# Layer 0's background steps re-spaced, and layer 1's first two convolution sums issued high products first

## The chip, the cores and the metric

The kernel runs on one core of a Trainium2 chip. The metric is the device time of one execution in microseconds (us). The profile has six rows of engines: PE (TensorE, matrix products), PEld (its weight loads), DVE (VectorE), ACT (ScalarE), POOL (GpSimd), and SP (SyncE, which here only issues transfers). Each works through its own list of instructions in order.

## The reference

Four layers on `x` of 16 images, 256 channels, 28x28 pixels. Only layers 0 and 1 matter here.

```python
# layer 0
out = _binary_activation(x)                       # the sign of x
scaling = mean(abs(weights), axis=(1, 2, 3))
bw = sign(weights)
y = _sat_conv2d(out, bw, padding=1) * scaling     # 3x3 convolution
yn = (y - mean(y)) * rsqrt(var(y) + EPS) * gamma + beta   # over all 16 images
x = yn + x
# layer 1
residual = prelu(x, a_alpha1)
z = hardsign(x + a_move)
y = conv_general_dilated(z, clip(a_w, -1, 1), padding=1)  # 3x3 convolution
y = prelu(bn(y, a_bn1), a_alpha2)
...                                               # gate, bn, 1x1 convolution, gate, bn
```

The normalization of layer 0 needs the mean and variance over all images. So layer 1 cannot begin before layer 0's last image has been convolved, evacuated and counted.

## The kernel before

**Layer 0** is `sign_layer` (line 322 on). Its blocks are images 0 to 14 whole and image 15 in three parts, a half and two quarters (15a, 15b, 15c). For a block j the kernel issues, in a hand-written order that holds for PE, ACT, DVE and SP alike:

1. `products(j)`: 36 matmuls of 392 columns for a whole image (line 340), on two weight rows packed into one value;
2. `sign_image(j+1)`: ACT writes the signs of the next image into one of two padded buffers `fpads` (line 451, two instructions), and SP issues the load of image j+4 (line 444; four buffers `xs`);
3. `post(j-1)`: DVE takes the statistics of the image before (line 598, four instructions), and POOL stores its integers `n` to memory (line 600);
4. two *slots* for a whole image, one for each part of image 15, from image 1 on: each slot takes the next entry of the list `steps`, and first runs what the entry before left over (`late`);
5. `apart(j)`: ACT rounds the sum in PSUM (lines 351 and 352), DVE separates the two packed rows (line 354). PSUM has three buffers for such sums.

The statistics of the first images are merged (`gather`, line 167) in the body of the first block whose part number is over 26, which is image 14.

**The list `steps`** is background work for later. Six times four entries prepare layer 1's and layer 2's weights: *taps* (DVE, lines 503 and 134, sums of three filter taps), *high* (ACT, line 514, four conversions to 16 bit; what it leaves over is *low*, line 518, four DVE instructions), *sum* (ACT, lines 285 and 288: absolute sum and sign sum of layer 0's weights; the last one leaves over the final sum on DVE, lines 294 and 295), and *sign* (ACT, line 266; leaves over one DVE instruction, line 267). Then comes *fw* (DVE line 302, ACT line 303, DVE line 134: layer 1's 1x1 weights), and `constants` (line 547 on): some 30 small DVE instructions and one ACT square root that fold layer 1's normalizations, and eight small SP loads of the gates' weights. Each of these entries issues the load of the entry two places further on (`load_ahead`); these loads share three buffers.

That is 26 entries. Images 1 to 14 and the three parts of image 15 have 2x14 + 3 = 31 slots. The entries therefore sit in the slots of images 1 to 13: odd images hold taps and high, even images sum and sign, image 13 holds fw and constants.

**Between the layers** `keep_busy(28)` (line 432) lets PE run 28 products on a buffer of zeros. `norm` (lines 184 and 134 to 148) makes scale and shift, `enter` (line 669, DVE) applies them to image 0, `sign1` (line 675, ACT) takes signs, `transform` (line 134, DVE, output `vs16`) makes the four row combinations u = 0 to 3 of a fast convolution in 16 bit, and `widen` (line 695, ACT) copies them to 32 bit (`vs`).

**Layer 1's convolution** is `conv` (line 713): for one u, six matmuls with the 16-bit *high* part of the weights on `vs16`, then six with the 32-bit *low* part on `vs`. `iteration(b)` begins with `conv_pair` for u = 1 and u = 2.

Of the kernel before, what the change touches and what calls it, by code (L numbers as in the profile page):

```python
# [34 lines left out]
ALU = mybir.AluOpType  # L35
# [8 lines left out]
HN = N // 2  # L44
# [39 lines left out]
def forward(ctx: ExitStack, tc: tile.TileContext, d: dict, out: bass.AP, careful: bool):  # L84
# [4 lines left out]
    V, A, T = nc.vector, nc.scalar, nc.tensor  # L89
# [11 lines left out]
    def pv(name):  # L101
        return vec[:, VECS.index(name), :]
# [30 lines left out]
    def tt(o, a, b, op):  # L133
        V.tensor_tensor(o, a, b, op)  # L134
        return o

    def rsqrt(name, v, half=None):

        r, t = (const.tile(list(v.shape), F32, name=name + q) for q in ("_r", "_t"))
        A.activation(t, v, AF.Sqrt)  # L140
        V.reciprocal(r, t)
        tt(t, r, r, ALU.mult)
        if half is not None:
            tt(r, r, half, ALU.mult)
        else:
            V.tensor_scalar(r, r, -0.5, None, ALU.mult)
        tt(t, t, v, ALU.mult)
        V.scalar_tensor_tensor(r, t, -3.0, r, ALU.add, ALU.mult)
        return r
# [98 lines left out]
    def load_ahead(steps, n, now=True):  # L248

        for s in steps[:n] if now else ():  # L250
            s.load()
        return [lambda s=s, t=t: (s.work(), t.load() if t else None)[0] for s, t in zip(steps, steps[n:] + [None] * n)]
# [143 lines left out]
    def combine(name, a, f, c=0.0):  # L396

        v = vtile(name)
        V.tensor_scalar(v, a, f, c, ALU.mult, ALU.add)
        return v  # L400
# [19 lines left out]
    with tc.tile_pool(name="ps_conv", bufs=3, space=PSUM) as psc, \  # L420
            tc.tile_pool(name="ps_sm", bufs=2, space=PSUM) as pss:

        def conv_ps():
            return psc.tile([P, 2, 512], F32, tag="cv", name="cv")
# [9 lines left out]
        with tc.tile_pool(name="ph1", bufs=1) as ph:  # L434
# [4 lines left out]
            def load_x(b, integers=False, rows=((0, S),)):  # L439
                if not xs[b]:  # L440
                    xs[b] = ph.tile([P, 2, N], F32, tag="xs", name=f"xs{b}", bufs=4)
                for r0, r1 in rows:
                    n = slice(r0 * S, r1 * S)
                    nc.sync.dma_start(out=xs[b][:, :, n], in_=d["x"][b][:, :, n])
                if integers:
                    ns[b] = ph.tile([P, 2, N], I16, tag="n", name=f"n{b}", bufs=2)
                    nc.sync.dma_start(out=ns[b], in_=n0d[b])
# [43 lines left out]
            w1 = [ph.tile([P, 2, 3, 4, 256], dt, name=f"w1_{i}") for i, dt in enumerate((HI, FR))]  # L491
# [32 lines left out]
            def fw_step():  # L524
                sts = []

                def load():
                    sts.append(xpool.tile([P, 3, 256], F32, tag="x2", name="stf", bufs=3))
                    nc.sync.dma_start(out=sts[0][:, 0:2, :], in_=d["fw"])

                return Step(load, lambda: split2(fw, sts[0][:, 0:2, :]))
# [5 lines left out]
            c1, c2, c3, c4 = (c_bn[:, i, :] for i in range(4))  # L537
            cc, zb2 = vtile("cc"), vtile("zb2")
            ra1, ra2, rf2, us1, ns1 = (vtile(q) for q in ("ra1", "ra2", "rf2", "us1", "ns1"))
            mix_x, mix_y, mix_c = (const.tile([P, 2, 2], F32, name=n) for n in ("mix_x", "mix_y", "mix_c"))  # L540
# [6 lines left out]
            def constants():  # L547
                for p in pads:
                    nc.gpsimd.memset(p, 0.0)
                nc.gpsimd.tensor_copy(  # L550
                    doubts[:, 4 * NB:4 * NB + 6], vec[:, VECS.index("a1"):VECS.index("a3") + 1, :].rearrange("p i k -> p (i k)")
                )
                for i, n in enumerate(("a_alpha2", "f_alpha2")):
                    nc.gpsimd.tensor_copy(doubts[:, 4 * NB + 6 + 2 * i:4 * NB + 8 + 2 * i], pv(n))
                v = const.tile([P, 4, 2], F32, name="v_bn")
                for i, bn in enumerate(bns):
                    V.tensor_scalar(v[:, 2 * i:2 * i + 2], bn[:, 3::4], EPS, None, ALU.add)
                r = rsqrt("bn", v)
                for i, bn in enumerate(bns):
                    two = slice(2 * i, 2 * i + 2)  # L560
                    tt(s_bn[:, two], bn[:, 0::4], r[:, two], ALU.mult)
                    tt(c_bn[:, two], bn[:, 2::4], s_bn[:, two], ALU.mult)
                    tt(c_bn[:, two], bn[:, 1::4], c_bn[:, two], ALU.subtract)
                tt(cc, c2, c4, ALU.add)

                for o, q in ((ra1, "a_alpha1"), (ra2, "a_alpha2"), (rf2, "f_alpha2")):
                    V.tensor_scalar(o, pv(q), -1.0, 1.0, ALU.mult, ALU.add)
                V.tensor_scalar(us1, s1, 1.0 / UP, None, ALU.mult)
                V.tensor_scalar(ns1, s1, -1.0 / UP, None, ALU.mult)
                tt(zb2, c2, pv("f_move"), ALU.add)  # L570
                for g, (q, scale) in enumerate((("a", pv("a_scale")), ("f", pv("f_scale")))):
                    V.tensor_scalar(mix_x[:, g], scale, 1.0 / N, None, ALU.mult)
                    V.tensor_scalar(mix_y[:, g], scale, -1.0 / N, 1.0 / N, ALU.mult, ALU.add)
                    rows = slice(32 * g, 32 * g + 32)
                    nc.sync.dma_start(out=w_1[:, :, rows], in_=d[f"se1_{q}"])
                    nc.sync.dma_start(out=w_2[rows], in_=d[f"se2_{q}"])
                    nc.sync.dma_start(out=b_1[rows], in_=d[f"seb_{q}"])
                    nc.sync.dma_start(out=w_2[64 + 32 * g:65 + 32 * g], in_=d[f"seb2_{q}"])
                tt(mix_c[:, 1], pv("f_scale"), c2, ALU.mult)

            w2a = packed_weights(wpool, tag="wa2")

# [3 lines left out]
            signs2, sums0 = sign_weights(xpool, w2a, d["w2a"], ("x2", 3), tmp=ph), weight_sums(room_sums, d["w0_rows"], sf0, 0)  # L586
            w1_steps = [w1_step(k, c) for k in range(2) for c in range(3)]
            ahead = load_ahead([t for s, *three in zip((w for w, _, _ in w1_steps), sums0, signs2) for t in (s, *three)] + [fw_step()], 2)
            steps = []
            for (_, high, low), taps, add_up, sign in zip(w1_steps, ahead[0::3], ahead[1::3], ahead[2::3]):  # L590
                steps += [taps, lambda high=high, low=low: (high(), low)[1], add_up, sign]
            steps += [ahead[-1], constants]

            def post0(block, ab):
                b, r0, rows = block
# [35 lines left out]
            vs = ph.tile([P, 2, 4, 2, HR, S + 2], FR, tag="vs", name="vs")  # L631
            vs16 = vs if careful else ph.tile([P, 2, 4, 2, HR, S + 2], BF16, name="vs16")
# [53 lines left out]
                )[u]  # L686
                tt(vs16[:, b % 2, u, k], x[:, k], y[:, k], op)

            def widen(b, u):

                if not careful:
                    v, w = (
                        t[:, b % 2, u].rearrange("p k i c -> p (k i c)") for t in (vs, vs16)
                    )
                    A.copy(v, w)  # L695

            rx = {}

# [5 lines left out]
                x = xs[b][:, k, :]  # L704
                V.scalar_tensor_tensor(x, rx.pop(k), ra1[:, k:k + 1], x, ALU.mult, ALU.add)

            def conv(b, mo, u, ps):

                n = 0
                for w, v in zip(w1, (vs16, vs)):  # L710
                    for k in range(2):
                        for c in range(3):
                            T.matmul(  # L713
                                ps.rearrange("p (a b) -> p a b", b=S),
                                lhsT=w[:, k, c, u, mo * P:(mo + 1) * P],
                                rhs=v[:, b % 2, u, k, :, c:c + S],
                                start=(n == 0),
                                stop=(n == 11),
                            )
                            n += 1  # L720


            uvs = wpool.tile([P, 2, 2, HN], F32, tag="wa", name="uvs")
# [1 line left out]
            pairs = {}  # L725

            def conv_pair(b, mo, i, u):
                if i == 0:
                    pairs[b, mo, u > 0 and u < 3] = conv_ps()
                conv(b, mo, u, pairs[b, mo, u > 0 and u < 3][:, i, :HN])  # L730

            def sum_pair_a(b, mo):
                t = temp("t1")[:, :HN]
                A.activation(
                    t, pairs[b, mo, True][:, 0, :HN], AF.Identity, bias=c1[:, mo:mo + 1], scale=us1[:, mo:mo + 1]
                )
                pairs[b, mo] = t
# [128 lines left out]
            def iteration(b):  # L866


                ahead, one, two = b + 1 < B, b >= 1, b >= 2
                if b + 2 < B:  # L870
                    xs[b + 2] = None
                    load_x(b + 2, True)
                for i, u in enumerate((1, 2)):
                    conv_pair(b, 0, i, u)
                if two:
                    unit_u(b - 2, 0)
                if two:
# [27 lines left out]
                if one:  # L905
                    g = gates(h)
# [59 lines left out]
            with tc.manual_schedule(engines={ET.PE, ET.DVE, ET.Activation}):  # L966
# [6 lines left out]
                for k in range(2):  # L973
                    for u in (1, 2):
                        transform(0, u, k)
                for u in (1, 2):
                    widen(0, u)
                nbi0 = combine("nbi0", bi0, -1.0)
                tt(mix_c[:, 0], pv("a_scale"), bi0, ALU.mult)
                for u in (0, 3):  # L980
# [10 lines left out]
                b = B - 1  # L991
                keep_busy(14)
                g = gates(hidden_b(B, hidden_a(B, px)))
# [47 lines left out]
                g = gates(h, dqg[:, 2])  # L1041
# [24 lines left out]
        with tc.tile_pool(name="ph2", bufs=1) as ph:  # L1066
# [76 lines left out]
            steps = []  # L1143
            if careful:
                steps = sign_weights(xpool, w2b, d["w2b"], ("x2", 3), tmp=ph)
# [5 lines left out]
                steps = [first_loads, None] + [t for s in load_ahead(steps, 2, now=False) for t in (None, None, s, None)]  # L1151
# [604 lines left out]
```

## Time and profile before

| what | value |
|---|---|
| median of the runs | 975.81 us (974.52 to 977.21, 3 runs) |
| the profiled execution's own time | 975.5 us |
| span of the profiled execution, first to last instruction | 973.7 us |
| PE, DVE, ACT, POOL busy over the span | 97%, 79%, 74%, 14% |
| PE busy, 22.0 to 52.5 us | 30.49 of 30.50 us |
| PE busy, 52.5 to 107.0 us (four stretches) | 49.59 of 54.50 us |
| last product of layer 0 ends, first product of layer 1 starts | 114.6 us, 123.15 us |
| transfers, 7 to 22 us, and 80.3 to 93.9 us | 403 GB/s, 278 GB/s |

Times in the trace count from the span's start. A row of the timeline gives the start, the length, the engine, the line, the operation, what it writes and reads, and how many instructions of the kind are merged. At its end, in brackets, stands how long the engine sat idle before it and what ended the wait. A row of the waits gives who waited for what, the total in us, how many times, and the longest.

### The profile page before, as it was taken

How to read it: one execution, taken by the hardware profiler on the slowest of the kernel's cores; microseconds unless marked ns; L12 is line 12 of the kernel's file. 1: busy time of each engine (PE TensorE's matmuls, PEld its weight loads, DVE VectorE, ACT ScalarE, POOL GpSimd, SP SyncE). 2: the span in 40 equal slices, each digit the busy share in tenths (PEclk: the TensorE clock that was granted, in tenths of full speed). 3: DMA queues.
4: the chain of work that ended last, by engine and by line, in shares of the span. 5: the costliest groups of instructions: out<-in, count | busy, mean ns of one | idle time of the engine just before them, and what ended most of it. 6: DMA issues, size and time to landing. Idle time of an engine off the chain costs nothing.

```text
span 973.7 us, 14804 instructions
## 1 busy us (share of the span) xinstructions
PE 944.8 (97%) x5615; PEld 582.8 (60%) x5615; DVE 773.4 (79%) x1417; ACT 722.3 (74%) x1199; POOL 141.0 (14%) x149
## 2 busy tenths in 40 slices
PE   7999899999999999999999999999999999999996
PEld 3555568877887878887555555555444444444443
DVE  4767878899998889985799997999757777777765
ACT  6787468888888888874788868887676767666652
POOL 3000100000000000000100000000054444444431
PEclk9999999999999999999999999999999999999998
DMA  9877513334443222110490000000044353525212
GB/s 347 312 271 270 197 50 99 116 115 131 146 152 117 100 100 96 58 63 34 180 383 1 1 1 1 1 1 1 1 71 96 72 129 70 130 67 133 67 67 103
DMA packets 26948, 105.82 MB, mean 109 GB/s; under 512 B 3490, under 2 KB 7268, under 8 KB 26868
## 3 DMA queue, kind: packets, MB, share of 16 engines
q1 hardware_dynamic: 20948, 73.44, 21.2%
q0 software_dynamic: 5632, 30.54, 11.6%
q8 instruction: 46, 0.75, 0.3%
q10 hardware_dynamic: 288, 0.80, 0.2%
q14 instruction: 34, 0.28, 0.1%
HBM read 72.67 MB, written 32.11 MB: 108 GB/s over the span
## 4 chain that ended last, share of the span: by engine, by line
PE 46%; DVE 3%; ACT 1%; issue 1%; DVEq 0%; ACTq 0%
PE cv L340 19%; PE sc L1331 8%; PE av L1352 8%; PE mi L1308 4%; PE sm L1394 2%; PE mi L1412 2%; PE sm L1352 1%; DVE p L1118 1%; DVE ab L354 0%; ACT es L1335 0%; DVE l2b_fin L1120 0%; DVE l2c_fin L1120 0%; DVE r L1378 0%; DVE p L1295 0%; PE sc L1412 0%
## 5 line engine op out<-in xcount | busy, mean ns | idle before, releaser
L340 PE MATMUL cv<-fpads,wpk 128*128 128x392 f16 (+1 forms) x1746 | 295.7, 331 | 10.2 <-ACT fpads L451 5.0
L713 PE MATMUL cv<-vs,w 128*128 128x392 bf16 (+1 forms) x1536 | 287.1, 356 | 2.9 <-DVE vs L134 2.7
L340 PEld LDWEIGHTS <-wpk 128*128 128x128 f16 x1746 | 169.0, 97 | 137.3 <-issue 9.9
L713 PEld LDWEIGHTS cv<-vs,w 128*128 128x128 f32 x768 | 142.6, 190 | 11.7 <-ACT vs L695 0.7
L1335 ACT ACTIVATE es<-sc 128x784 f32<-128x784 f32 x112 | 87.3, 822 | 41.4 <-PE sc L1331 41.4
L713 PEld LDWEIGHTS <-w 128*128 128x128 f16 x768 | 67.7, 101 | 58.1 <-issue 18.5
L1331 PE MATMUL sc<-q,keyswa 64*128 64x392 f32 x448 | 89.9, 513 | 0.9 <-ACT es L1335 0.9
L1118 DVE SCALAR_TENSOR_TENSOR p<-ab,vec 128x392 f32<-128x392 f32 x128 | 79.1, 618 | 2.3
L1352 PE MATMUL av<-es,v 128*64 128x392 f32 x448 | 80.7, 499 | 0.0
L1345 POOL TENSOR_TENSOR sum<-sum,es 128x784 f32<-128x784 f32 x32 | 67.2, 2100 | 3.1 <-ACT es L1335 0.6
L1331 PEld LDWEIGHTS sc<-q,keyswa 64*128 64x128 f32 x448 | 38.9, 186 | 44.0 <-issue 17.1
L851 POOL DMA_DIRECT2D x2d<-x x16 | 8.6, 537 | 343.9 <-DVE x L845 280.9
L1319 DVE COPY keyswa<-mi 64x392 f32<-64x392 f32 x31 | 16.3, 564 | 52.6 <-ACT q L1315 52.5
L1352 PEld LDWEIGHTS av<-es,v 128*64 128x64 f32 x448 | 29.4, 136 | 47.4 <-issue 47.0
L695 ACT CAST vs<-vs 128x840 fp32r<-128x840 bf16 x64 | 54.7, 882 | 1.5 <-DVE vs L134 1.5
L351 ACT ACTIVATE t<-cv,rounding 128x392 f32<-128x392 f32 (+2 forms) x82 | 51.6, 630 | 4.9 <-PE cv L340 1.9
L1123 ACT ACTIVATE t<-ab 128x392 f32<-128x392 f32 x64 | 33.5, 524 | 27.9 <-DVE ab L354 27.9
L823 PE MATMUL cv<-z,fw 128*128 128x392 f32 x256 | 48.9, 342 | 1.0 <-ACT z L815 0.8
L354 DVE SCALAR_TENSOR_TENSOR ab<-ab,cv 128x392 f32<-128x392 f32 x64 | 35.5, 554 | 17.5 <-ACT ab L352 17.5
L823 PEld LDWEIGHTS cv<-z,fw 128*128 128x128 f32 x256 | 45.7, 188 | 2.3 <-ACT z L815 2.1
L1308 PE MATMUL mi<-p,wqk 128*128 128x392 f32 x124 | 45.3, 506 | 0.3 <-DVE p L1295 0.3
L432 PE MATMUL unused<-idle 128*128 128x512 bf16 x175 | 40.5, 389 | 3.0 <-POOL idle L468 3.0
(287 smaller groups left out, 1511.4 us busy)
## 6 DMA issues: line engine op xcount, KB each, us to landing
xs<-in_x_dram SPq DMA_DIRECT2D x30, 784.0 KB, 5.8
x2d<-x POOLq DMA_DIRECT2D x16, 784.0 KB, 3.8
out_dram<-p SPq DMA_DIRECT2D x15, 784.0 KB, 3.8
p<-x2d POOLq DMA_DIRECT2D x14, 784.0 KB, 6.9
p<-x2d SPq DMA_DIRECT2D x13, 784.0 KB, 16.1
n0d<-n POOLq DMA_DIRECT2D x16, 392.0 KB, 4.7
n<-n0d SPq DMA_DIRECT2D x16, 392.0 KB, 3.3
st<-in_w_dram SPq DMA_DIRECT2D x12, 384.0 KB, 6.1
```

What stands on the lines that cost most here:

```text
L340: T.matmul(pss[j][:, n // size if careful else h, :rows * S].rearrange("p (a b) -> p a b", b=S), lhsT=w[:, n, t, :], rhs=pads[:, blocks[j] ...
L351: A.activation(by_halves(t, blocks[j]), ps, AF.Identity, bias=rounding, scale=1.0 / PACK)
L432: tc.keep_in_program_order(T.matmul(ps, lhsT=idle[:, 0:P], rhs=idle, start=True, stop=True))
L695: A.copy(v, w)
L713: T.matmul(ps.rearrange("p (a b) -> p a b", b=S), lhsT=w[:, k, c, u, mo * P:(mo + 1) * P], rhs=v[:, b % 2, u, k, :, c:c + S], start=(n == ...
L823: T.matmul(ps[:, h, :HN], lhsT=w[:, k, mo * P:(mo + 1) * P], rhs=z2[b][:, k, h * HN:(h + 1) * HN], start=(k + i == 0), stop=(k + i == 2),)
L1118: V.scalar_tensor_tensor(p, y, alpha[:, mo:mo + 1], y, ALU.mult, ALU.max)
L1308: T.matmul(ps[:, h, :HN], lhsT=wqk[:, k, :], rhs=x[b][:, k, h * HN:(h + 1) * HN], start=(k == 0), stop=(k == 1))
L1331: T.matmul(ps[:, h, :HN], lhsT=chunk[rows], rhs=qs[b][rows], start=True, stop=True)
L1335: A.activation(e, ps[:, :, :HN], AF.Exp, scale=0.125)
L1345: (V if late else nc.gpsimd).tensor_tensor(sums[b, late], sums[b, late], e, ALU.add)
L1352: T.matmul(ps[64 * h:64 * h + 64, :HN], lhsT=w, rhs=e[:, h, :], start=start, stop=stop)
```

## The change

Four edits.

- `constants` loses its eight loads, which become an entry of their own, `gate_weights`. `constants` moves to the front of `steps`, `gate_weights` stands at its end: 27 entries.
- Four empty entries are put between weight entries, so that all 31 slots are used.
- `conv` takes a list of parts (0: high, 1: low). The first two sums of layer 1 (image 0, first 128 output channels, u = 1 and 2) are issued as high u1, high u2, low u1, low u2.
- Of image 0's first two `widen` copies the second (u = 2) goes to DVE (`tensor_copy`) instead of ACT.

```diff
@@ constants @@
                     V.tensor_scalar(mix_y[:, g], scale, -1.0 / N, 1.0 / N, ALU.mult, ALU.add)
+                tt(mix_c[:, 1], pv("f_scale"), c2, ALU.mult)
+
+            def gate_weights():
+                for g, q in enumerate("af"):
                     rows = slice(32 * g, 32 * g + 32)
                     nc.sync.dma_start(out=w_1[:, :, rows], in_=d[f"se1_{q}"])
                     nc.sync.dma_start(out=w_2[rows], in_=d[f"se2_{q}"])
                     nc.sync.dma_start(out=b_1[rows], in_=d[f"seb_{q}"])
                     nc.sync.dma_start(out=w_2[64 + 32 * g:65 + 32 * g], in_=d[f"seb2_{q}"])
-                tt(mix_c[:, 1], pv("f_scale"), c2, ALU.mult)
@@ the list of steps @@
-            steps = []
+            steps = [constants]
             for (_, high, low), taps, add_up, sign in zip(w1_steps, ahead[0::3], ahead[1::3], ahead[2::3]):
                 steps += [taps, lambda high=high, low=low: (high(), low)[1], add_up, sign]
-            steps += [ahead[-1], constants]
+            steps += [ahead[-1], gate_weights]
+            for i in (21, 17, 13, 9):
+                steps[i:i] = [None]
@@ widen, conv @@
-            def widen(b, u):
+            def widen(b, u, copy=A.copy):
-                    A.copy(v, w)
+                    copy(v, w)
-            def conv(b, mo, u, ps):
-
-                n = 0
-                for w, v in zip(w1, (vs16, vs)):
+            def conv(b, mo, u, ps, parts=range(2)):
+
+                for part in parts:
+                    w, v = w1[part], (vs16, vs)[part]
                     for k in range(2):
                         for c in range(3):
...
-                                start=(n == 0),
-                                stop=(n == 11),
+                                start=((part, k, c) == (0, 0, 0)),
+                                stop=((part, k, c) == (1, 1, 2)),
                             )
-                            n += 1
+            def first_pair():
+                ps = pairs[0, 0, True] = conv_ps()
+                for part in range(2):
+                    for i, u in enumerate((1, 2)):
+                        conv(0, 0, u, ps[:, i, :HN], (part,))
@@ iteration, start of layer 1 @@
-                for i, u in enumerate((1, 2)):
-                    conv_pair(b, 0, i, u)
+                if b == 0:
+                    first_pair()
+                else:
+                    for i, u in enumerate((1, 2)):
+                        conv_pair(b, 0, i, u)
...
-                for u in (1, 2):
-                    widen(0, u)
+                widen(0, 1)
+                widen(0, 2, V.tensor_copy)
```

After the change the slots hold, by image (– is an empty entry): 1 constants, taps; 2 high, sum; 3 sign, taps; 4 high, sum; 5 sign, –; 6 taps, high; 7 sum, sign; 8 –, taps; 9 high, sum; 10 sign, –; 11 taps, high; 12 sum, sign; 13 –, taps; 14 high, sum; 15a sign; 15b fw; 15c the gates' loads.

## Prediction

> **What bounds the kernel now.** I read the list of waits over layer 0 first. PE's sum there has one entry that comes back:
>
> ```profile
> PE cv L340 <- ACT fpads L451: 5.0, 5, 1.1
> ACT w L514 <- DVE st L503: 14.4, 6, 2.5
> ```
>
> Five times PE waits for the signs of the next image, and six times ACT waits for DVE's taps. The timeline over two images (here 11 and 12) shows how the second makes the first:
>
> ```profile
> 79.47 1.59 ACT L451 ACTIVATE fpads<-xs 128x784 f16<-128x784 f32 x2
> 80.36 12.39 PE L340 MATMUL cv<-fpads,wpk 128*128 128x392 f16 x72 [1.14 <-ACT fpads L451]
> ...
> 80.96 0.83 ACT L285 ACTIVATE sts<-sts 128x768 f32<-128x768 f32 x1
> ...
> 82.75 0.83 ACT L266 ACTIVATE sg<-st 128x768 bf16<-128x768 f32 x1
> ...
> 83.49 0.89 ACT L351 ACTIVATE t<-cv,rounding 128x784 f32<-128x784 f32 x1
> ...
> 85.27 1.59 ACT L451 ACTIVATE fpads<-xs 128x784 f16<-128x784 f32 x2
> ...
> 89.33 0.42 ACT L514 ACTIVATE w<-st 128x256 f16<-128x256 f32 x1 [2.47 <-DVE st L503]
> ...
> 91.22 0.90 ACT L351 ACTIVATE t<-cv,rounding 128x784 f32<-128x784 f32 x1
> ...
> 93.00 1.59 ACT L451 ACTIVATE fpads<-xs 128x784 f16<-128x784 f32 x2
> ```
>
> PE needs 12.39 / 2 = 6.20 us per image. ACT needs 5.80 for one (79.47 to 85.27) and 7.73 for the other (85.27 to 93.00), because taps and high stand in the same image and ACT sits idle 2.47 us between them. Together that is 13.53, against 12.39 on PE: 1.14 us lost per two images.
>
> ACT may be late by some amount first. `apart` can't start before PE has finished its image; it takes 1.78 (83.49 to 85.27), the signs follow, and PE starts 0.89 after them (79.47 to 80.36). So ACT can lag by 6.20 - 1.78 - 0.89 = 3.53 us before PE stops. The odd images add 7.73 - 6.20 = 1.53 to the lag and the even ones take 0.40 off: from image 1 on that is 3.81 after image 5, and there the first gap comes (0.80, before image 7). From then on each pair's 1.14 is a gap: before images 9, 11 and 13, and 0.76 before image 15. Ahead of image 7 PE runs without a gap, so image 2 begins at 52.49 - 5 x 6.20 = 21.5.
>
> The third view is the timeline between the layers:
>
> ```profile
> 107.32 0.96 DVE L354 SCALAR_TENSOR_TENSOR n<-n,cv 128x784 int16<-128x784 int16 x1
> ...
> 111.90 0.97 DVE L354 SCALAR_TENSOR_TENSOR n<-n,cv 128x784 int16<-128x784 int16 x1
> ...
> 118.17 0.56 DVE L184 BATCH_NORM_AGGREGATE l_mv<-l_fin 128x2 f32<-128x45 f32 x2
> ...
> 123.15 0.68 PE L713 MATMUL cv<-vs,w 128*128 128x392 bf16 x3 [2.47 <-DVE vs L134]
> ```
>
> DVE has no gap from 104.5 (constants, then image 13's line 354 at 107.32) to the final statistics at 118.17. PE (image 14 done at 106.29) is not the bound there. After 124.98 PE has no gap above 0.08 us until 451.8, so layer 1 is bound by PE, and what layer 1 starts earlier it ends earlier.
>
> **Part 1: the order of the steps.** It removes nothing; it moves. ACT's cost per image: signs 1.49 (79.47 to 80.96), sum 1.79, sign 0.74, `apart` 1.78, four highs about 1.3 if they needn't wait (0.33 from one to the next; my estimate). With the new slots:
> - high and sum: 1.49 + 1.31 + 1.79 + 1.78 = 6.37, lag +0.17;
> - sign with taps or nothing: 4.0; nothing with taps: 3.3; the lag goes to 0;
> - taps and high together (images 6, 11): about 7.2 (7.73 less the line 267, 0.5, that no longer stands before the taps), lag +1.0;
> - sum and sign after them (7, 12): 5.80, lag -0.4.
>
> The largest lag is 1.2 us, far below 3.53. The gaps before images 7 to 13 go: 0.80 + 3 x 1.14 = 4.22 us. Image 14 ends at 106.29 - 4.22 = 102.05. The gap before image 15 goes too, but DVE decides there.
>
> Constants in image 1 cost DVE about 3.3 us (103.99 to 107.32) and ACT one 0.21 square root. DVE then reaches image 1's line 354 about 1 us later than now; PE needs that buffer only three images later (18 us). That is the cover, and it costs nothing.
>
> **The tail, step by step**, from PE's end of image 13 at 95.85. ACT rounds image 13 until 97.7. DVE: line 354 to 98.8, statistics (1.9) to 100.65, gather (1.6 and 0.17) to 102.4, four lows (0.33 each) to 103.7. ACT: signs to 99.1, highs to 100.4, sum to 102.2, image 14's rounding to 104.0. DVE: line 354 to 105.1, statistics 107.0, final sum 0.4 to 107.4, 15a's line 354 to 107.95, 0.2, statistics 1.0 to 109.1, line 267 to 109.55, fw's line 302 to 110.0, two small ones to 110.4, the wait for ACT's copy (0.65) to 110.7, line 134 to 111.3, 15b (waits for ACT until 111.5) 111.9, 112.45, 15c 112.8, 113.37. So the final statistics start at 113.37, not 118.17: **4.80 us earlier**. That is 4.22 from PE and 0.58 from 3.3 us of constants that left, less what sum, sign and fw now put into DVE's tail.
>
> Transfers moved with it: the last taps' load now stands behind layer 1's first two image loads in SP's list, and fw's behind two more. Fw's load can go out when the last sum is done (102.2); DVE wants it at 109.55, so it has 7.3 us. Landings of SP's loads after 28 us in this trace took 3.6 to 9.2 us, and the load of fw itself, issued 96.41, less than 5.9. I take 0, and keep up to 9.2 - 7.3 = 1.9, or by the longest landing of all (10.7, early in the layer) 3.4. The taps want theirs at 95.7, about 6 us after issue; 1.5 us late costs under 1, since DVE waits for image 13 until 97.7 anyway. The eight gate loads take SP 4.3 us (96.84 to 101.13), done by about 107; image 0's integers can be reloaded from 109 on (its buffer is stored 3.6 after 105.3) and are wanted at 115.3.
>
> **Part 2: the first pair.** Before, PE waits 0.22 (line 134) and then 0.26 for ACT's first 32-bit copy (line 695). Now six high products of u2 (over 1 us) stand in between, so the 0.26 goes and the 0.22 stays. The copy on DVE has no row with this form: at least 0.55 (line 503, 768 elements), at most 1.03 (line 669, two inputs); starting at 124.3 it is done by 125.4 while PE wants it after 126.8, so either end costs nothing. It delays `transform` u0 and u3 by as much; PE wants those after 24 products, at 130.8, against 126.9. **-0.26 us**.
>
> Sum: 975.5 - 4.80 - 0.26 = **970.4 us**. The profiled execution lies 0.3 below the median, so I leave it.
>
> **A price with a doubt: the clock.** PE's granted clock is 0.50 from about 125.3 to 128.7, after the 2.47 us gap; a matmul then takes 0.33 instead of 0.17 to 0.19, some 1.7 us lost. The 28 idle products now end at 114.75 (15c ends 108.55, plus 6.2) and layer 1 begins at 118.35: the gap grows to 3.6 us. I take the same single stretch, so no difference. [...]
>
> **The rivals.**
> - *Two half-speed stretches* (or one and a part) after the longer gap. For: the gap grows by 1.1 us. Against: the gap of 2.47 gave one. Time: 970.4 + 1.7 = 972.1. Chance 0.12. No half-speed at work: 968.7, chance 0.07.
> - *Late transfer*: fw lands 9.2 to 10.7 us after issue, DVE stops at line 302 with all of image 15 behind it: 972.3 to 973.8. Against: three loads at most ahead of it. Chance 0.08.
> - *Slower*: the empty slots don't free ACT. If ACT's two-image cost stays above PE's 12.39, the gaps stay (+4.22) and the full lag of 3.53 reaches image 14, whose rounding then stands 3.3 us later than worked out, ahead of the sign and fw work that is now last: 970.4 + 4.22 + 3.3 = 977.9. It decides when the lag at image 14 passes 3.53; by the rows it is 0.2. Chance 0.05.
> - *The change doesn't do what it says*: loads bound the layer, and PE waits for images instead. 403 GB/s were reached from 7 to 22 us; from 22 to 107 the sum over my stretches is 24 MB in 85 us, which in 80.5 us is 300 GB/s. It would end within 0.3% of now, about 974.5. Chance 0.03.
> - *The forecast* as summed keeps 0.65.
>
> **How the numbers follow.** About 0.3% (2.9 us) can be told from no change: 972.9 is the edge. Faster: the forecast, no half-speed, most of two stretches, a part of the late transfer, 0.85. Within: the rest of these and the load-bound case, 0.10. Slower: 0.05. The range must hold the clock (1.7 either way) and a late transfer of up to about 3: 968.2 to 973.4.
>
> **What would show it.** Right: no PE gap from the signs above 0.1 us between 22 and 102; image 14 done near 102; the final statistics near 113.4; the first product of layer 1 near 118.4; no wait for line 695's first copy; constants' square root near 21. Wrong: DVE idle before line 302 or 503 with a transfer as the cause; ACT still late at image 14; granted clock at half for more than 3.4 us after 118.

## The result, and the profile after

The changed kernel takes 968.95 us (median of 4 runs, 967.72 to 970.32); the kernel before took 975.3 us (median of 4, the three runs given above among them). The ratio is 0.9933, 95% interval 0.9916 to 0.9951: faster by 0.7%. The forecast was 970.4 us within 968.2 to 973.4.

| place | before | after | difference |
|---|---|---|---|
| largest PE gap from the signs in layer 0, 20 to 108 us | 1.14 us, five gaps | none over 0.08 us | |
| image 14 separated by DVE (line 354) | 111.90 | 103.76 | -8.14 |
| final statistics (line 184) | 118.17 | 112.72 | -5.45 |
| first product of layer 1 | 123.15 | 117.69 | -5.46 |
| its first 24 products take | 6.80 | 6.32 | -0.48 |
| last product of layer 1's 3x3 convolution starts | 458.18 | 452.23 | -5.95 |
| span | 973.7 | 967.7 | -6.0 |

All of it arises before 125 us; layer 1 is bound by PE, and from there on the two executions run side by side.

The list of waits over layer 0, after, answers to the first view of before:

```profile
ACT t L351 <- PE cv L340: 9.5, 7, 1.9
...
ACT w L514 <- DVE st L503: 4.0, 2, 2.0
...
PE cv L340 <- ACT fpads L451: 0.2, 1, 0.2
```

The wait of PE for signs has shrunk from 5.0 us to a single 0.2, early in the layer. ACT waits for taps twice instead of six times (images 6 and 11, the only ones that still hold taps and high together). And an entry that was 1.0 us, once, before shows who leads now: ACT waits seven times for PE to finish its products. It is no longer late.

The timeline around image 6 shows the largest lag that is left:

```profile
51.99 0.42 ACT L514 ACTIVATE w<-st 128x256 f16<-128x256 f32 x1 [2.01 <-DVE st L503]
...
53.87 0.90 ACT L351 ACTIVATE t<-cv,rounding 128x784 f32<-128x784 f32 x1
55.65 1.59 ACT L451 ACTIVATE fpads<-xs 128x784 f16<-128x784 f32 x2
```

ACT's idle time before the highs is 2.01 us here, against 2.47: the line 267 no longer stands in front. ACT rounds image 6 at 53.87; PE has finished it at about 52.7 (46.6, where ACT waited for image 5, plus one image). So the lag is 1.2 us, and PE would stop only at about 3.5.

The timeline between the layers, after (line numbers move with the edits: the convolution of layer 1 is line 713 before, 718 here and 716 in some of the runs below):

```profile
97.46 0.97 DVE L354 SCALAR_TENSOR_TENSOR n<-n,cv 128x784 int16<-128x784 int16 x1
...
103.76 0.97 DVE L354 SCALAR_TENSOR_TENSOR n<-n,cv 128x784 int16<-128x784 int16 x1 [0.30 <-ACT n L352]
...
108.94 0.42 DVE L302 TENSOR_SCALAR stf<-stf 128x512 f32<-128x512 f32 x1
...
110.05 0.69 DVE L134 TENSOR_TENSOR fw<-stf,fw 128x512 fp32r<-128x512 f32 x1 [0.41 <-ACT fw L303]
...
112.72 0.56 DVE L184 BATCH_NORM_AGGREGATE l_mv<-l_fin 128x2 f32<-128x45 f32 x2
...
117.69 0.68 PE L718 MATMUL cv<-vs,w 128*128 128x392 bf16 x3 [3.87 <-DVE vs L134]
```

Image 14 is separated 8.1 us earlier (4.7 from PE's gaps, the rest because fw and constants no longer stand in image 13, where DVE fell behind), but the final statistics come only 5.45 earlier. Between them DVE now takes 8.96 us instead of 6.27: the last sums, the line 267 and fw (108.94 to 110.74, with 0.41 of waiting for ACT's copy) have moved in there. No bracket stands before line 302, so fw's transfer was in time. The gap on PE has grown from 2.47 to 3.87 us, and one half-speed stretch follows it (118.6 to 122.0), as before.

### The profile page after: what moved, and what is told of

It reads as the page before. It is cut to its first block, busy times and chain, and to the rows that moved or that the text cites. A ratio compares the mean times of both kernels' runs of the same rounds, so it can differ in the third digit from the quotient of the medians.

```text
span 967.7 us, 14795 instructions
## 1 busy us (share of the span) xinstructions
PE 942.3 (97%) x5609; PEld 582.1 (60%) x5615; DVE 773.8 (80%) x1418; ACT 721.7 (75%) x1198; POOL 140.9 (15%) x149
## 4 chain that ended last, share of the span: by engine, by line
PE 46%; DVE 3%; ACT 1%; issue 1%; DVEq 0%; ACTq 0%
PE cv L340 19%; PE sc L1344 8%; PE av L1365 8%; PE mi L1321 4%; PE sm L1407 2%; PE mi L1425 2%; PE sm L1365 1%; DVE p L1131 1%; DVE ab L354 0%; ACT es L1348 0%; DVE l2b_fin L1133 0%; DVE l2c_fin L1133 0%; DVE r L1391 0%; DVE p L1308 0%; DVE p L1307 0%
## 5 line engine op out<-in xcount | busy, mean ns | idle before, releaser
L1356 POOL TENSOR_TENSOR sum<-es 128x784 f32<-128x784 f32 x16 | 30.0, 1877 | 91.0 <-ACT es L1348 91.0
```

## The experiments

**Each part alone.**

The edits are given against the changed kernel: steps_only takes back the pair and the copy, pair_only takes back the list of steps (constants and the loads last, no empty entries).

```diff
-                if b == 0:
-                    first_pair()
-                else:
-                    for i, u in enumerate((1, 2)):
-                        conv_pair(b, 0, i, u)
+                for i, u in enumerate((1, 2)):
+                    conv_pair(b, 0, i, u)
...
-                widen(0, 1)
-                widen(0, 2, V.tensor_copy)
+                for u in (1, 2):
+                    widen(0, u)
```

```diff
-            steps = [constants]
+            steps = []
...
-            steps += [ahead[-1], gate_weights]
-            for i in (21, 17, 13, 9):
-                steps[i:i] = [None]
+            steps += [ahead[-1], lambda: (constants(), gate_weights())[1]]
```

> The first part alone: the new list of steps, with layer 1's first pair issued as before and both first copies on ACT. My theory (ACT's lag goes because taps and high no longer stand in the same image every second time): no PE gap from the signs, the final statistics at 112.7 us and the first product of layer 1 at 117.7 as after the whole change; the first 24 products take 6.8 us as before, not 6.3. Time 968.95 + 0.5 = 969.4 us. Rival (a good part comes from the pair): over 971.

> The second part alone: the first pair with high products first and one copy on DVE, the list of steps as before. My theory: the PE gaps of layer 0 stay as they were, the first 24 products of layer 1 take 6.3 us instead of 6.8. Time 975.3 - 0.5 = 974.8 us. Rival (a good part comes from the pair): under 973.

Measured: 969.02 us for the steps alone (ratio 0.9932, 0.9915 to 0.9948) and 974.63 for the pair alone (0.9989, 0.9979 to 1.0000). The steps are nearly the whole gain: first product at 117.82, no gap from the signs. In the profile of pair_only the gaps are still there (0.46, 1.14, 1.14, 1.14 before images 7 to 13, and 0.76 before image 15); by its interval the pair's gain is at the edge of what can be told from nothing. What was expected of the first 24 products missed in both: 7.07 us instead of 6.8 with the old pair, 4.71 instead of 6.3 with the new one. The granted clock differs in just these stretches: in steps_only a half-speed stretch of 6.83 us reached 5.9 us past the restart, and in pair_only none fell there (it lay at 10.5 to 13.9 us). So the pair needed a run without that.

**One empty entry in the kernel before.** Taps and high are parted by shifting the list one slot; constants stay last.

```diff
-            steps = []
+            steps = [None]
```

> The kernel before with a single empty entry ahead of its list of steps and nothing else changed: constants stay last, the pair is as before. It shifts the list by one slot, so that taps stand at the end of one image and high at the start of the next. My theory (the pairing of taps and high in one image is the cause): all PE gaps from the signs go, as with the whole change. Constants now stand in image 14 behind the merging of the statistics, 3.3 us of DVE on its path, but sum, sign and fw are done by image 13: final statistics at about 111.7 us against 112.7, and 968.95 - 1.0 + 0.5 = 968.4 us. Rival 1 (the gain is the constants' way out of the tail): about 975. Rival 2 (it takes the empty entries between the weight steps): the gaps stay, about 975.

Measured: 969.04 us (0.9929, 0.9915 to 0.9943), first product at 117.35, final statistics 0.7 us ahead of the changed kernel's. The waits of this run:

```profile
ACT t L351 <- PE cv L340: 13.2, 8, 2.3
ACT bn_t L140 <- DVE v_bn L557: 3.4, 1, 3.4
...
PE cv L340 <- DVE n L354: 0.7, 1, 0.7
```

There is no line for PE waiting for signs. One entry gives the time of the whole change. Both rivals fall: constants are last here, and no entry stands between the weight steps. The new 0.7 is PE waiting for a PSUM buffer that DVE frees late, because constants now sit in front of image 14's separation. About half of the 0.7 us that the final statistics gain is lost again: DVE waits 0.38 us for image 0's reloaded integers, and the first product is 0.34 us ahead.

**Taps and high paired again.** The changed kernel, with one empty entry behind constants instead of the four.

```diff
-            steps = [constants]
+            steps = [constants, None]
...
-            for i in (21, 17, 13, 9):
-                steps[i:i] = [None]
```

> The changed kernel with one empty entry behind constants instead of the four: the list starts constants, empty, taps, high, so taps and high stand in one image again, in images 2, 4 to 12, as in the kernel before one image later. My theory (the pairing is the cause): the gaps come back, before images 8, 10, 12 and 14, about 0.8 and 1.1 us each, and what constants no longer cost in the tail is given back by fw, which now stands in image 14: about 975 us, although constants come first, an empty entry is there and the pair is the new one. Rival 1 (constants' way out of the tail is the gain): 969 to 971.

Measured: 975.24 us, ratio 0.9999 (0.9988 to 1.001): the gain is gone, with constants first and the new pair in place. The waits show what came back:

```profile
ACT w L514 <- DVE st L503: 14.9, 6, 2.5
...
PE cv L340 <- ACT fpads L451: 4.3, 4, 1.1
...
PE cv L340 <- DVE n L354: 3.1, 1, 3.1
```

Four gaps of 0.86 to 1.15 us, before images 8, 10, 12 and 14, as forecast one image later. The tail shows how a late ACT and late work add up: fw stands before image 14's separation, which comes later than in the kernel before (111.90):

```profile
113.00 0.97 DVE L354 SCALAR_TENSOR_TENSOR n<-n,cv 128x784 int16<-128x784 int16 x1 [1.10 <-ACT n L352]
```

So the way back to 975 us is not the gaps alone. The final statistics come at 119.27, 6.55 us later than in the changed kernel; the four gaps are 4.3 of that by their rows, and the rest is this tail.

**The empty entries alone.** The kernel before, with four empty entries ahead of the last four taps; constants come in 15b.

```diff
             steps += [ahead[-1], constants]
+            for i in (20, 16, 12, 8):
+                steps[i:i] = [None]
```

> The kernel before with the four empty entries alone, ahead of the last four taps: constants and the loads stay at the end and so come in 15b, the pair is as before. Theory: taps and high share an image only four times with room between, the lag stays under 3.5 us and no gap comes from the signs; but constants' 3.3 us of DVE now lie behind fw with the last quarter waiting: final statistics near 116.2 instead of 112.6, and 968.95 + 3.5 + 0.4 = 972.9 us. Rival (constants' place is worth nothing): 969.4.

Measured: 975.04 us (0.9989, 0.9979 to 0.9999), 2.1 us above what I expected. The mechanism is there: no gap from the signs, and the last products of layer 0 end as early as after the change (the idle products begin at 107.58). What I undersized is the tail:

```profile
105.01 0.97 DVE L354 SCALAR_TENSOR_TENSOR n<-n,cv 128x784 int16<-128x784 int16 x1
...
112.16 0.22 DVE L557 TENSOR_SCALAR v_bn<-vec 128x4 f32<-128x4 f32 x2
...
115.47 0.35 DVE L354 SCALAR_TENSOR_TENSOR n<-n,cv 128x196 int16<-128x196 int16 x1
...
117.32 0.56 DVE L184 BATCH_NORM_AGGREGATE l_mv<-l_fin 128x2 f32<-128x45 f32 x2
```

Constants take DVE from 112.16 to 115.47 with the last quarters waiting, 3.3 us as expected; but image 14's separation is also 1.25 us later than after the change (105.01 against 103.76). Image 13's is already 0.75 later (98.21 against 97.46), since taps and high stand together in image 13 here, and the last sum and the small operations behind it fall in front of image 14's. The final statistics stand at 117.32, 4.6 us later than after the change and 1.1 later than I expected. The clock at the restart does not explain the rest of the 2.1: PE idles 8.5 us and restarts at half speed for 4.5 us, but its first 24 products take 6.38 us, against 6.32 after the change. About 0.6 us is lost at the end of the program, where this profile has a half-speed stretch (963.0 to 966.4) that the changed kernel's has not; what remains no profile shows. So freeing PE is worth nothing by itself here if DVE's work moves behind the last image.

**No empty entries.** The changed kernel without its four.

```diff
-            for i in (21, 17, 13, 9):
-                steps[i:i] = [None]
```

> The changed kernel without its four empty entries: constants first, then the 24 weight entries without a space, fw and the gates' loads. My theory: constants ahead shift the list by one slot, which parts taps from high in every image, so no gap comes back; and all the work is done by image 14, so that sum, sign, low and fw leave DVE's tail. Final statistics at about 109.9 us instead of 112.7: 966.1 us. The gap ahead of layer 1 shrinks to about 1 us (15c ends near 107.5, plus 6.2 us of idle products, first product near 114.8); if the half-speed stretch goes with it, 1.7 us less, 964.4. Rival 2 (the empty entries are needed): PE gaps come back, 972 or more.

Measured: 964.8 us (0.9890, 0.9874 to 0.9906), and 964.84 when measured again. It beats both kernels. The tail in its timeline:

```profile
97.84 0.97 DVE L354 SCALAR_TENSOR_TENSOR n<-n,cv 128x784 int16<-128x784 int16 x1 [1.10 <-ACT n L352]
...
103.38 0.97 DVE L354 SCALAR_TENSOR_TENSOR n<-n,cv 128x784 int16<-128x784 int16 x1 [0.88 <-ACT n L352]
...
109.65 0.56 DVE L184 BATCH_NORM_AGGREGATE l_mv<-l_fin 128x2 f32<-128x45 f32 x2
...
114.63 0.68 PE L716 MATMUL cv<-vs,w 128*128 128x392 bf16 x3 [1.01 <-DVE vs L134]
```

DVE waits for ACT before images 13 and 14, so it has room; from image 14 to the final statistics it needs 6.27 us, as in the kernel before. The statistics are 3.07 us ahead of the changed kernel's, and the PE gap of 1.01 us brings no half-speed stretch: the first 24 products take 4.71 us, not 6.32. Together that is 4.7 us, of the 5.0 between the two spans and the 4.15 between the medians.

> The kernel without empty entries once more, beside the one with both copies on ACT on the same chip. Expected as before: 4.7 us for the first 24 products, 964.8 us.

**The pair at full clock.** The same kernel with the pair and copies as before the change, and with the new order but both copies on ACT.

The first takes back pair and copy as steps_only does, the second the copy alone:

```diff
-                widen(0, 1)
-                widen(0, 2, V.tensor_copy)
+                for u in (1, 2):
+                    widen(0, u)
```

> The kernel without empty entries (964.8 us), with the first pair and both copies as before the change. There the gap ahead of layer 1 is 1.0 us and no half-speed stretch follows, so the pair can be seen at full clock: 4.7 us for the first 24 products with the new pair. Theory: the wait for ACT's first 32-bit copy comes back, 5.1 us for the 24 products, 965.2 us. Rival (the new pair does nothing beyond the clock's shifts): 4.7 and 964.8.

> The kernel without empty entries and with high products first, but both first copies on ACT as before. ACT's second copy would be done about 1.75 us after its first began, while PE then still has to do most of the six high products of u2 and the six low ones of u1. Theory (the order of the products is the whole gain of the pair): the first 24 products take 4.7 us, 964.8 us. Rival (the copy on DVE is needed): 5.0 us or more, 965.1.

Measured: 965.17 us (0.9897, 0.9880 to 0.9914) with the old pair, its first 24 products in 5.24 us; 964.81 us (0.9886, 0.9863 to 0.9909) with the new order and both copies on ACT, 4.71 us. The order saves 0.53 us by the profiles; the copy's engine makes no difference. The medians differ by 0.4 us, which is less than the runs of one kernel spread, so the size rests on the profiles. The wait that the order takes away stands in the last row of the run with the old pair:

```profile
115.97 2.48 ACT L698 CAST vs<-vs 128x840 fp32r<-128x840 bf16 x3 [0.44 <-DVE vs L134]
115.98 0.67 PE L716 MATMUL cv<-vs,w 128*128 128x392 bf16 x3 [0.21 <-DVE vs L134]
...
116.91 1.41 PE L716 MATMUL cv<-vs,w 128*128 128x392 f32 x6 [0.26 <-ACT vs L698]
```

With the new pair (the run without empty entries) PE waits once more, before its fourth product, and not before the seventh:

```profile
115.53 2.64 PE L716 MATMUL cv<-vs,w 128*128 128x392 bf16 x14 [0.21 <-DVE vs L134]
```

**The clock.** The changed kernel with 43 idle products between the layers instead of 28.

```diff
-            keep_busy(28)
+            keep_busy(43)
```

> The changed kernel with 43 idle products between the layers instead of 28: 15 more at 0.22 us fill 3.3 of the 3.9 us gap ahead of layer 1 (the last would end near 117.1, the first product stands at 117.7). Theory (the gap brings the half-speed stretch): no granted clock of 0.5 after 117, the first 24 products take 4.7 us instead of 6.3: 968.95 - 1.6 = 967.3 us. [...]

Measured: 967.64 us, first product at 117.62 after a gap of 0.61 us, first 24 products in 4.71 us. Ratio to the kernel before: 0.9918 (0.9904 to 0.9932). The rows of the windows for 120 to 122 us, first of the changed kernel and then of this run. They give the window and its length, then busy time and, in brackets, instructions of PE, PEld, DVE, ACT and POOL, then the granted clock, the DMA share and GB/s:

```profile
120.00:122.00 2.00, 2.00 (x8) 1.29 (x6) 0.61 (x2) 1.86 (x3) 0.00 (x0) 0.50 0.00 0
```

```profile
120.00:122.00 2.00, 2.00 (x13) 1.98 (x12) 0.54 (x2) 1.94 (x3) 0.00 (x0) 1.00 0.00 0
```

PE reads as fully busy in both, but does 8 products in the one and 13 in the other. Without the long gap the stretch is gone, which is worth 1.6 us by the profiles and 1.3 by the medians. One profile alone could be chance, since pair_only had a gap of 2.77 us and no stretch behind it; the last section counts the others.

## Why the prediction was right, point by point

- **What bounds layer 0**: right. The chain from taps and high in one image, over ACT's lag, to PE's gaps is shown from both sides: parting them by one empty entry in the kernel before removes the gaps, pairing them again in the changed kernel brings them back.
- **The gaps are worth 4.22 us**: right in kind, small in size. Image 13's first product stands at about 89.2 (image 1 begins at 15.80, and twelve images of 6.12 follow without a gap) against 93.89: 4.7. I took PE's time per image from the busy row, 12.39 / 2 = 6.20; by ACT's waits for PE (22.11, 34.35, 46.59, 64.94, 77.18, 95.53) an image takes 6.12. A product of line 340 has a row of 0.33 us, but the products start 0.17 apart (on average over 20 to 50 us, in both kernels); so a busy row reads about 0.15 longer than that pace gives, and each gap behind it about 0.15 short. With 6.12 the sum of the lag comes closer as well: ACT's 7.73 and 5.80 then give a lag of 4.2 after image 5, PE stops at 3.45, and the first gap would be 0.75, where the row shows 0.80. The 3.81 and 3.53 of the prediction would have given 0.28, which it did not compare with the row.
- **The lag stays under 3.53**: right. 1.2 us after images 6 and 11, 0.2 at image 14, as worked out.
- **Constants in image 1 cost nothing**: right. DVE separates image 1 at 26.30 instead of 25.45; no one waits.
- **The tail ends 4.80 earlier**: 5.45. Image 14's separation ended at 104.73, 0.4 before the 105.1 worked out, by the faster PE. From there to line 302 DVE took 4.2 us instead of the 4.45 added up, because each step had been rounded up a little. Fw's round trip over ACT took what was forecast.
- **Transfers in time**: right. Fw, issued 101.97, was used at 108.94 without a wait; the last taps landed at 94.43 and were used at 95.53; image 0's integers at 111.85, used at 114.67.
- **The pair -0.26**: 0.48 between the two profiles, 0.53 at full clock. The same mistake in small: between the sixth and seventh start in the kernel before lie 0.58 us, 0.40 more than a product takes, where the list of waits shows 0.26. What the last 0.1 is, no run shows. (The 24 products end at 129.94 in the kernel before, not at 130.8 as I read; that leaves the copy on DVE 3 us.) That the copy on DVE has no price was right; it took 0.60 us, inside the bounds.
- **One half-speed stretch**: right in the profiled pair of runs, and partly luck. With a stretch behind the gap the first 24 products take 6.32 us in the changed kernel, and 6.36, 6.38, 6.80 and 7.07 in four profiles with the old pair; in pair_only, after 2.77 us, none fell there and they take 4.71. The runs of steps_only spread from 968.32 to 971.48.

Before to after, the forecast had 4.80 + 0.26 = 5.06 us; the profiles show 6.0. The missing 0.9 is 0.65 in layer 0 and its tail, 0.22 in the pair, and less than 0.1 after it. About half of it comes from busy rows read as PE's time, and another 0.24 is the tail's steps rounded up. What I did not see is that the change is two steps with opposite signs: moving constants ahead already parts taps from high, and the four empty entries then cost about 4 us, the clock included, by pushing the last weights into DVE's tail.

## What to carry to other kernels

When background work is dealt out in slots, its order within a slot can matter more than its place: look for a slot in which one engine must wait for another's part of the same step, and compare the engine's time per cycle with that of the engine that bounds. Empty slots are not free: what they push behind the last block lies on the path to whatever needs that block. And count the time per item from start to start, or from who waits for it, not from the busy row: here that is 6.12 us per image, against 6.20 by the row.

## What the hardware showed beyond that

Half-speed stretches that begin and end within an execution were 3.41 us long in the profiles of both kernels (125.41 to 128.82 before, 118.63 to 122.05 after), 6.83 in that of steps_only and 10.24 in that of empties_only (116.5 to 126.7): once, twice and three times the same number, at different places. After gaps of 0.61 to 1.12 us between the idle products and layer 1 (six profiles) none reached the first products; after 2.47 to 8.49 us one did in five profiles and missed in one. In the run with taps and high paired again PE stood still 3.10 us before the last quarter of image 15, and a stretch began 0.9 us after that gap; the 1.12 us ahead of layer 1 brought none. In the kernel before, a gap of 2.47 us, with 0.22 and 0.26 between the products behind it, was followed by one. What sets the place and the length of a stretch, no run shows.
